# Transposing h and h2 with block DMAs and VectorE instead of TensorE, in a two-layer graph kernel on one core

## The chip, the core and the metric

The kernel runs on one core of one Trainium2 chip. The metric is the device time of one execution in microseconds, lower is better. "Before" and "after" are the medians of several executions. A run of a program on a single core is called fast unless it lies more than 1.5% above the fastest of the same kernel; all runs quoted here are fast ones.

## The reference, cut to what matters

Layer 0 normalizes x, applies a three-hop diffusion with attention weights and adds the result; layer 1 normalizes again and adds a gated value projection. B = 128 graphs, N = 128 nodes, D = 512 features, all fp32.

```python
h = jnp.maximum(_layernorm(x), 0.0)                    # "h" in the kernel
# layer 0
e = leaky_relu(sj[:, None, :] + si[:, :, None] + ab)    # sj, si from h @ Wv
transition = A * exp(e) / (sum(A * exp(e), -1) + 1e-12)
H = 0; Xk = h
for k in range(3):
    H = H + Xk @ Wk[k] + bk[k]
    Xk = transition @ Xk
x = x + relu(H)
# layer 1
h = jnp.maximum(_layernorm(x), 0.0)                    # "h2" in the kernel
q, k = split(h @ Wqk); v = h @ Wv
w = inv_scale * mask * sum(q * (adj @ (k * mask)), -1)
x = x + softmax(w, axis=1)[:, :, None] * v
```

## The kernel before

Two graphs form a pair, and there are 64 pairs. The products of a layer contract over features, and the kernel hands h and h2 to TensorE with the features on the partitions. Each layer is done as seven block products in the manner of Strassen: three banks of PSUM, each used twice or three times, with evictions on VectorE in between that set free the bank for its next product. Layer 1 of a pair runs after layer 0 of the next pair. The parts that the change touches:

```python
def transposed(h, dst):                      # h [128 nodes, 2 graphs, 512] -> features on partitions
    for j in range(G):
        pt = ps_t.tile([P, 2, HC, P], FP, name="pt")
        for c in range(DC):
            nc.tensor.transpose(pt[:, c // HC, c % HC, :], h[:, j, c * P:(c + 1) * P], ident)   # L239
        (nc.vector.tensor_copy if j else nc.scalar.copy)(dst(j), pt)                            # L240

def strassen0(p, steps):                     # layer 0; [cut: evictions of the first products]
    ...
    product(bb, 6, True)
    nc.vector.tensor_add(s[:, 2], b, s[:, 1])
    steps[0]()                               # next pair: transposed(h), attention
    product(bc, 7, True)
    product(bb, 5, False)
    nc.vector.tensor_add(s[:, 3], b, s[:, 0])          # L339 before, L360 after
    nc.vector.tensor_add(hb[:, 1, HD:], c, s[:, 3])
    steps[1]()
    product(ba, 2, False)
    nc.vector.tensor_add(hb[:, 0, :HD], a, lo)
    product(bb, 3, False)                    # reuses the bank that L339 / L360 reads
    ...

def strassen1(p):                            # layer 1
    product(a, 1, True)
    nc.scalar.copy(s[:, 0], a)
    product(b, 6, True)
    nc.vector.tensor_add(s[:, 1], b, s[:, 0])          # L364 before, L385 after
    product(c, 7, True)
    product(b, 5, False)                     # reuses the bank that L364 / L385 reads
    ...

for p in range(NP + 1):                      # [cut: first and last pairs]
    strassen0(p, steps)                      # steps: transposed(h[p+1]), attention(p+1), ...
    propagate(p + 1)
    H2[p] = norm_relu(X1[p], "h2", late["p"])
    yv = strassen1(p - 1)
    w = aggregate(p - 1, yv)
    prepare0(p + 1)
    finish(p - 1, yv, w)                     # softmax of pair p-1 and its output
    X2[p] = late["p"].tile([P, G, 2, HC, N], FP, name="x2")
    transposed(H2[p], lambda j: X2[p][:, j])
    SX2[p] = left_sums(...)                  # four sums that products 5, 6, 7, 3 need
    norm0(p + 2)
```

In the traces of this case VectorE and the queues took their instructions in the order in which a scheduler laid them down when the kernel was built, not in the order of the source. That will matter.

## Time and profile before

| | before |
|---|---|
| time, median (3 runs) | 2529.99 us (2529.98 to 2530.89) |
| TensorE busy | 99% of the span |
| one steady period (a pair) | 38.49 us |
| VectorE work in a period | 26.2 us |
| mean granted clock of TensorE | 0.995 |

In the views, PE is TensorE, PEld its weight loads, DVE VectorE, ACT ScalarE and SPq the DMA queue of the sync engine; `out<-in` names the tiles that an instruction writes and reads, and `<-` after an idle time names what ended it. The prediction below shows and reads the busy table, the chain of waits and the timeline. The first is the view of cores; the second the view by source line of the adjacency load's DMA, where the three numbers are the shortest, median and longest time in ns that an issue held its queue.

```profile
core 0: 2528.2 us, clock 0.995
```

```profile
L70 SPq DMA_DIRECT2D ag<-in_adj_dram x64: 367/368/459, 1.2 to 2327.0; - x64
```

This load out of DRAM held the queue for 0.37 us in the median, 0.46 at the most. L240 copied the transposes of h and h2 out of their `pt` tiles, 128 times on VectorE at 675 ns and 128 times on ScalarE at 586.

### The profile page before, as it was taken

What the parts mean: (1) busy time and instruction counts of PE and PEld (TensorE: products, weight loads), DVE (VectorE), ACT (ScalarE), POOL (GpSimd) and SP (SyncE); (2) the same over time, 40 slices, a digit from 0 to 9 for tenths busy, and PEclk for the clock granted to TensorE, in tenths of its full rate; (3) what the DMA queues carried; (4) which work ended last, traced back from release to release, by engine and by line L of the source; (5) the groups of instructions that cost most, each with busy time, mean ns of one, the idle gap of its engine ahead of it and who ended that gap; (6) DMA issues with size and microseconds to landing.
All of it is one profiled execution on the core that took longest, in us unless ns stands there. A gap on an engine that the chain in (4) does not pass through costs nothing.

```text
span 2528.2 us, 28170 instructions
## 1 busy us (share of the span) xinstructions
PE 2491.1 (99%) x10313; PEld 1794.9 (71%) x10313; DVE 1700.4 (67%) x4648; ACT 698.6 (28%) x1677; POOL 0.7 (0%) x6
## 2 busy tenths in 40 slices
PE   5999999999999999999999999999999999999998
PEld 4677676776776776776767767767767767677675
DVE  6666667667667666666676676676666666766764
ACT  2322222223223223222222232232232222222321
POOL 0000000000000000000000000000000000000000
PEclk8999999999999999999999999999999999999999
DMA  5110010001000100100100010001001001000000
GB/s 161 36 38 30 28 38 29 29 30 36 30 30 28 38 30 28 38 30 28 38 28 30 30 36 30 30 28 38 30 28 38 30 27 36 30 30 30 34 9 25
DMA packets 62473, 86.28 MB, mean 34 GB/s; under 512 B 3712, under 2 KB 28416, under 8 KB 62336
## 3 DMA queue, kind: packets, MB, share of 16 engines
q1 hardware_dynamic: 62336, 84.49, 10.1%
q8 instruction: 81, 1.33, 0.2%
q14 instruction: 56, 0.46, 0.1%
HBM read 50.92 MB, written 33.55 MB: 33 GB/s over the span
## 4 chain that ended last, share of the span: by engine, by line
PE 96%; issue 0%; DVE 0%; ACT 0%; DVEq 0%; ACTq 0%
PE pm L313 75%; PE pt L293 8%; PE pt L239 4%; PE pt L383 4%; PE pt L124 1%; PE pt L281 1%; PE pt L277 1%; PE pt L266 1%; ACT h L216 0%; DVE junk L386 0%; DVE x L409 0%; ACT ej L400 0%; DVE yv L374 0%; DVEq L478 0%; DVE w L397 0%
## 5 line engine op out<-in xcount | busy, mean ns | idle before, releaser
L313 PE MATMUL pm<-t,sx 128*128 128x256 f32 x2304 | 518.6, 379 | 0.1
L313 PEld LDWEIGHTS pm<-t,sx 128*128 128x128 f32 x2304 | 432.6, 190 | 56.4 <-DVE sx L302 0.3
L313 PE MATMUL pm<-b,x 128*128 128x256 f32 x1536 | 390.8, 380 | 0.0
L313 PE MATMUL pm<-f,sx 128*128 128x512 f32 x768 | 340.1, 592 | 0.0
L313 PEld LDWEIGHTS pm<-b,x 128*128 128x128 f32 x1536 | 267.6, 191 | 55.2 <-issue 30.1
L295 ACT COPY x<-pt 128x512 f32<-128x512 f32 x256 | 147.6, 576 | 488.3 <-PE pt L293 488.3
L313 PEld LDWEIGHTS pm<-f,sx 128*128 128x128 f32 x768 | 145.6, 190 | 184.2 <-issue 150.2
L313 PE MATMUL pm<-e,x 128*128 128x512 f32 x512 | 240.6, 592 | 0.0
L293 PE MATMUL pt<-tt,h 128*128 128x256 f32 x1024 | 233.9, 382 | 0.5 <-ACT tt L282 0.5
L293 PEld LDWEIGHTS pt<-tt,h 128*128 128x128 f32 x1024 | 196.1, 192 | 27.9 <-ACT tt L282 0.8
L216 ACT ACTIVATE h<-x,rs 128x512 f32<-128x512 f32 x128 | 97.3, 807 | 290.1 <-PE pt L383 278.5
L313 PE MATMUL pm<-b,sx 128*128 128x256 f32 x768 | 176.2, 379 | 0.0
L313 PE MATMUL pm<-t,x 128*128 128x256 f32 x768 | 176.2, 379 | 0.0
L231 DVE SCALAR_TENSOR_TENSOR junk<-h,u_bc 128x512 f32<-128x512 f32 x256 | 174.4, 684 | 1.8 <-ACT h L216 1.8
L313 PEld LDWEIGHTS pm<-e,x 128*128 128x128 f32 x512 | 97.3, 190 | 95.6 <-issue 92.1
L313 PEld LDWEIGHTS pm<-b,sx 128*128 128x128 f32 x768 | 145.9, 190 | 19.8
L313 PEld LDWEIGHTS pm<-t,x 128*128 128x128 f32 x768 | 145.9, 190 | 19.8
L216 ACT ACTIVATE h<-xg,rs 128x512 f32<-128x512 f32 x128 | 97.1, 806 | 175.3 <-DVE rs L213 175.3
L239 PE MATMUL pt<-ident,h 128*128 128x128 f32 x1024 | 144.7, 274 | 0.7 <-ACT h L216 0.5
L240 ACT COPY x<-pt 128x512 f32<-128x512 f32 x128 | 75.1, 586 | 248.1 <-PE pt L239 242.3
L239 PEld LDWEIGHTS pt<-ident,h 128*128 128x128 f32 x1024 | 122.6, 142 | 14.1 <-ACT h L216 1.4
L372 DVE TENSOR_TENSOR yv<-pm,s 128x512 f32<-128x512 f32 x64 | 44.3, 692 | 129.0 <-PE pm L313 129.0
(105 smaller groups left out, 2844.9 us busy)
## 6 DMA issues: line engine op xcount, KB each, us to landing
xg<-in_x_dram SPq DMA_DIRECT2D x64, 512.0 KB, 3.5
out_dram<-x SPq DMA_DIRECT2D x64, 512.0 KB, 2.8
ag<-in_adj_dram SPq DMA_DIRECT2D x64, 128.0 KB, 2.1
b<-in_L_gnn_Wk_dram SPq DMA_DIRECT2D x12, 256.0 KB, 5.9
w<-in_L_gnn_Wqk_dram SPq DMA_DIRECT2D x8, 256.0 KB, 5.3
wv_sb<-in_L_gnn_Wv_dram SPq DMA_DIRECT2D x1, 1024.0 KB, 7.5
e<-in_L_gnn_Wv_dram SPq DMA_DIRECT2D x4, 256.0 KB, 6.1
bk_bc<-in_L_gnn_bk_dram SPq DMA_DIRECT2D x3, 256.0 KB, 5.8
```

The costliest lines, as they stand in the source:

```text
L124: nc.tensor.transpose(dst, col.to_broadcast([P, P]), ident)
L216: nc.scalar.activation(h[:, j, :], src[:, j, :], AF.Relu, bias=rs[:, 1, j:j + 1], scale=rs[:, 0, j:j + 1])
L231: nc.vector.scalar_tensor_tensor(junk, h[:, j, :], 1.0, u_bc[:, a, :], op0=OP.mult, op1=OP.mult, accum_out=s[:, j, a:a + 1])
L239: nc.tensor.transpose(pt[:, c // HC, c % HC, :], h[:, j, c * P:(c + 1) * P], ident)
L240: (nc.vector.tensor_copy if j else nc.scalar.copy)(dst(j), pt)
L266: nc.tensor.transpose(pa[:, j, :], a[:, j, :], ident)
L277: nc.tensor.transpose(pt[:, j, :], t[:, j, :], ident)
L293: nc.tensor.matmul(pt[:, c].rearrange("p k n -> p (k n)"), h[:, j, at:at + P], tt[:, j].rearrange("p k n -> p (k n)"), start=True, stop=True)
L295: nc.scalar.copy(X[p][:, j, kh, 1:3].rearrange("p k c n -> p c k n"), pt)
L313: nc.tensor.matmul(bank[:, :width], left[i][:, c * P:(c + 1) * P], right[i][:, c], start=(first and c == 0), stop=(c == n - 1), skip_group ...
L372: nc.vector.tensor_add(o[0][1], b, s[:, 0])
L383: nc.tensor.matmul(pa, at[:, j, :], h2[:, j, :], start=True, stop=True)
```

## The change

The intent is to take the transposes off TensorE, the engine that bounds the kernel (96% of the chain that ended last). DMAs move 32-row blocks between partitions, in runs of 512 bytes, and VectorE finishes the transposition within blocks of 32x32. The features then come out in a permuted order, and the rows of the weights are loaded in the same order to match. Besides, the softmax of a pair (`finish`) is moved into layer 0 of the pair after next, where its two small matmuls need not wait for VectorE (before, their weight loads waited 20.4 us in all).

```diff
     def transposed(h, dst):
-        for j in range(G):
-            pt = ps_t.tile([P, 2, HC, P], FP, name="pt")
+        hv = front.tile([P, Q, G, P], FP, name="hv", bufs=1)
+        for n in range(Q):                                   # Q = 4, DC = 4: 16 DMAs
             for c in range(DC):
-                nc.tensor.transpose(pt[:, c // HC, c % HC, :], h[:, j, c * P:(c + 1) * P], ident)
-            (nc.vector.tensor_copy if j else nc.scalar.copy)(dst(j), pt)
+                nc.sync.dma_start(hv[c * S32:(c + 1) * S32, n],              # L255
+                                  h[n * S32:(n + 1) * S32, :, c * P:(c + 1) * P])
+        for j in range(G):
+            nc.vector.transpose(dst[:, j].rearrange("p f (n b) -> p f n b", n=Q),   # L258
+                                hv[:, :, j].rearrange("p n (f a) -> p f n a", f=Q))
...  (weight rows loaded in the permuted order; layout of x; one junk buffer instead of two)
-                steps = (lambda: (begin(n), attention(n)), lambda: t_transposed(n))
+                steps = (lambda: (begin(n), attention(n), end()), lambda: t_transposed(n))
...
-            finish(p - 1, yv, w)
+            ends.append((p - 1, yv, w))                      # end() calls finish later
```

More of the change, by code (lines that the diff above doesn't have):

```diff
@@ L44 @@
     G = 2
+    S32 = 32
+    Q = P // S32
     NP = B // G
@@ L88, with rows @@
     nc.sync.dma_start(nm, nodemask)
+    def rows(dst, w, kh):
+        for c in range(DC):
+            at = c * P + kh * HC * S32
+            nc.sync.dma_start(dst[c * S32:(c + 1) * S32],
+                              w[at:at + HC * S32].rearrange("(f a) o -> a f o", a=S32))
     def block0(pool, name, kh, nh):
         t = pool.tile([P, K, HC, HD], FP, name=name)
-        for k in range(K):
+        rows(t[:, 0], wk[0, :, nh * HD:(nh + 1) * HD], kh)
+        for k in range(1, K):
             src = wk[k, kh * HD:(kh + 1) * HD, nh * HD:(nh + 1) * HD]
@@ L113 @@
             e[kh, nh] = pool.tile([P, HC, 2, HD], FP, name=f"e{kh}{nh}")
-            src = wv1[kh * HD:(kh + 1) * HD, nh * HD:(nh + 1) * HD]
-            nc.sync.dma_start(e[kh, nh][:, :, 1, :], src.rearrange("(c p) o -> p c o", p=P))
+            rows(e[kh, nh][:, :, 1, :], wv1[:, nh * HD:(nh + 1) * HD], kh)
     ident = const.tile([P, P], FP, name="ident")
@@ L131 @@
         for c in range(DC):
-            junk = front.tile([P, D], FP, name="junk")
+            junk = front.tile([P, D], FP, name="junk", bufs=1)
             nc.vector.scalar_tensor_tensor(junk, wv0_sb[:, c, :], 1.0, aw_bc[:, a, :],
@@ L138 @@
         nc.vector.tensor_copy(u_bc[:, a, :], pu.rearrange("p c i -> p (c i)"))
-        junk = front.tile([P, D], FP, name="junk")
+        junk = front.tile([P, D], FP, name="junk", bufs=1)
         nc.vector.scalar_tensor_tensor(junk, bv_bc, 1.0, aw_bc[:, a, :],
@@ L184, in score_matrix @@
                 t = wpool.tile([P, D], FP, name=f"wt{a}")
-                (nc.vector.tensor_copy if a else nc.scalar.copy)(t, p.rearrange("p c i -> p (c i)"))
+                if a:
+                    nc.vector.tensor_copy(t, p.rearrange("p c i -> p (c i)"))
+                else:
+                    nc.scalar.copy(t.rearrange("p (f c a) -> p f c a", f=Q, c=DC),
+                                   p.rearrange("p c (f a) -> p f c a", f=Q))
                 wt.append(t)
@@ L229, in norm0 @@
             for a in range(2):
-                junk = front.tile([P, D], FP, name="junk")
+                junk = front.tile([P, D], FP, name="junk", bufs=1)
                 nc.vector.scalar_tensor_tensor(junk, h[:, j, :], 1.0, u_bc[:, a, :], op0=OP.mult,
@@ L234, in transposed @@
     def transposed(h, dst):
+        hv = front.tile([P, Q, G, P], FP, name="hv", bufs=1)
+        for n in range(Q):
+            for c in range(DC):
+                nc.sync.dma_start(hv[c * S32:(c + 1) * S32, n],
+                                  h[n * S32:(n + 1) * S32, :, c * P:(c + 1) * P])
         for j in range(G):
-            pt = ps_t.tile([P, 2, HC, P], FP, name="pt")
-            for c in range(DC):
-                nc.tensor.transpose(pt[:, c // HC, c % HC, :], h[:, j, c * P:(c + 1) * P], ident)
-            (nc.vector.tensor_copy if j else nc.scalar.copy)(dst(j), pt)
+            nc.vector.transpose(dst[:, j].rearrange("p f (n b) -> p f n b", n=Q),
+                                hv[:, :, j].rearrange("p n (f a) -> p f n a", f=Q))
     def attention(p):
@@ L294, in propagate @@
                                      tt[:, j].rearrange("p k n -> p (k n)"), start=True, stop=True)
-                nc.scalar.copy(X[p][:, j, kh, 1:3].rearrange("p k c n -> p c k n"), pt)
-    def left_sums(blocks, pool, name, width, bufs):
-        s = pool.tile([P, 4, width], FP, name=name, bufs=bufs)
-        a = [[blocks[:, j, kh] for kh in range(2)] for j in range(G)]
-        nc.vector.tensor_add(s[:, 0], a[1][0], a[1][1])
-        nc.vector.tensor_sub(s[:, 1], s[:, 0], a[0][0])
-        nc.vector.tensor_sub(s[:, 2], a[0][0], a[1][0])
-        nc.vector.tensor_sub(s[:, 3], a[0][1], s[:, 1])
+                nc.scalar.copy(X[p][:, 1:3, j, kh].rearrange("p k c n -> p c k n"), pt)
@@ L305, in left_sums @@
+    def left_sums(a, pool, name, width):
+        s = pool.tile([P, 4] + width, FP, name=name, bufs=1)
+        nc.vector.tensor_add(s[:, 0], a[1, 0], a[1, 1])
+        nc.vector.tensor_sub(s[:, 1], s[:, 0], a[0, 0])
+        nc.vector.tensor_sub(s[:, 2], a[0, 0], a[1, 0])
+        nc.vector.tensor_sub(s[:, 3], a[0, 1], s[:, 1])
         return dict(zip((5, 6, 7, 3, 1, 2, 4),
-                        [s[:, 0], s[:, 1], s[:, 2], s[:, 3], a[0][0], a[0][1], a[1][1]]))
-    def products(left, right, width):
+                        [s[:, 0], s[:, 1], s[:, 2], s[:, 3], a[0, 0], a[0, 1], a[1, 1]]))
@@ L310, in product, with products @@
+    def products(left, right):
         def product(bank, i, first):
-            n = left[i].shape[1] // P
-            for c in range(n):
-                nc.tensor.matmul(bank[:, :width], left[i][:, c * P:(c + 1) * P], right[i][:, c],
-                                 start=(first and c == 0), stop=(c == n - 1), skip_group_check=True)
+            _, n, m = left[i].shape
+            chunks = [(k, c) for k in range(n) for c in range(m // P)]
+            for at, (k, c) in enumerate(chunks):
+                r = right[i][:, k, c]
+                nc.tensor.matmul(bank[:, :r.shape[-1]], left[i][:, k, c * P:(c + 1) * P], r,
+                                 start=(first and at == 0), stop=(at == len(chunks) - 1),
+                                 skip_group_check=True)
@@ L315, in products @@
         return product
-    R0 = {i: t.rearrange("p k c o -> p (k c) o") for i, t in right0.items()}
     def prepare0(p):
-        SX[p] = left_sums(X[p].rearrange("p j h k c n -> p j h (k c n)"), front, "sx", K * HD, 1)
+        a = {(j, kh): X[p][:, :, j, kh].rearrange("p k c n -> p k (c n)")
+             for j in range(G) for kh in range(2)}
+        SX[p] = left_sums(a, front, "sx", [K, HD])
     def strassen0(p, steps):
-        product = products(SX.pop(p), R0, HD)
+        product = products(SX.pop(p), right0)
@@ L353, in strassen1 @@
     def strassen1(p):
-        product = products(SX2.pop(p), R1, D)
+        product = products(SX2.pop(p), R1)
         X2.pop(p)
@@ L383, in aggregate @@
             nc.tensor.matmul(pa, at[:, j, :], h2[:, j, :], start=True, stop=True)
-            junk = front.tile([P, D], FP, name="junk")
+            junk = front.tile([P, D], FP, name="junk", bufs=1)
             b = p * G + j
@@ L413, in begin @@
     def begin(p):
-        X[p] = front.tile([P, G, 2, K, HC, N], FP, name="x")
-        transposed(H[p], lambda j: X[p][:, j, :, 0])
-    nothing = (lambda: None, lambda: None)
+        X[p] = front.tile([P, K, G, 2, HC, N], FP, name="x")
+        transposed(H[p], X[p][:, 0].rearrange("p j h c n -> p j (h c) n"))
     norm0(0)
@@ L425, with end @@
     R1 = None
-    W = {}
+    ends = []
+    def end():
+        while ends:
+            finish(*ends.pop())
     for p in range(NP + 1):
@@ L430 @@
                 n = p + 1
-                steps = (lambda: (begin(n), attention(n)), lambda: t_transposed(n))
+                steps = (lambda: (begin(n), attention(n), end()), lambda: t_transposed(n))
             else:
-                steps = nothing
+                steps = (end, lambda: None)
             strassen0(p, steps)
@@ L436 @@
                 propagate(p + 1)
+        else:
+            end()
         if p == 0:
@@ L439 @@
             setup_ctx.close()
-            R1 = {i: t.rearrange("p c k o -> p c (k o)") for i, t in right1.items()}
+            R1 = {i: t.rearrange("p (s c) k o -> p s c (k o)", s=1) for i, t in right1.items()}
             late["p"] = ctx.enter_context(tc.tile_pool(name="late", bufs=1))
@@ L449 @@
         if p > 0:
-            finish(p - 1, yv, w)
+            ends.append((p - 1, yv, w))
         if p < NP:
             X2[p] = late["p"].tile([P, G, 2, HC, N], FP, name="x2")
-            transposed(H2[p], lambda j: X2[p][:, j])
-            SX2[p] = left_sums(X2[p].rearrange("p j h c n -> p j h (c n)"), late["p"], "sx2", HD, 1)
+            transposed(H2[p], X2[p].rearrange("p j h c n -> p j (h c) n"))
+            a = {(j, kh): X2[p][:, j, kh:kh + 1].rearrange("p k c n -> p k (c n)")
+                 for j in range(G) for kh in range(2)}
+            SX2[p] = left_sums(a, late["p"], "sx2", [1, HD])
         if p + 2 < NP:
             norm0(p + 2)
+    end()
 _INS = ['x', 'adj', 'nodemask', 'L0_gnn_Wv', 'L0_gnn_bv', 'L0_gnn_aw', 'L0_gnn_ab', 'L0_gnn_Wk',
```

## The prediction

Its 0.65 us for a transpose of 512 elements a partition on VectorE is the author's estimate: the trace before had other work of that size at 0.68 us, with the next start after 0.6, and no such transpose.

> **What bounds the kernel now.** I read the busy table of the page first, then the chain of waits that ended last, then the timeline of one pair in the middle of the run.
>
> ```profile
> PE 2491.1 (99%) x10313; PEld 1794.9 (71%) x10313; DVE 1700.4 (67%) x4648; ACT 698.6 (28%) x1677; POOL 0.7 (0%) x6
> ...
> PE 96%; issue 0%; DVE 0%; ACT 0%; DVEq 0%; ACTq 0%
> PE pm L313 75%; PE pt L293 8%; PE pt L239 4%; PE pt L383 4%; PE pt L124 1%; PE pt L281 1%; PE pt L277 1%; PE pt L266 1%; ACT h L216 0%; DVE junk L386 0%; DVE x L409 0%; ACT ej L400 0%; DVE yv L374 0%; DVEq L478 0%; DVE w L397 0%
> ...
> L239 PE MATMUL pt<-ident,h 128*128 128x128 f32 x1024 | 144.7, 274 | 0.7 <-ACT h L216 0.5
> ```
>
> TensorE carries 96% of the chain. L239, the transposes of h and h2, is 4% of it, about 100 us; that is what the change takes away. Busy time alone would mislead, because matmul records overlap. So I took distances between starts in a steady stretch:
>
> ```profile
> 1206.25 1.04 PE L239 MATMUL pt<-ident,h 128*128 128x128 f32 x8
> 1207.12 0.38 PE L124 MATMUL pt<-ident,s 128*128 128x128 f32 x2
> ```
>
> Eight transposes occupy 0.87 us, or 0.109 us each, not the 274 ns of the row. The two groups of four in the same pair take 0.43 us each, so one pair (8 for h2, 8 for h) spends 1.73 us. The same way: 84 records of 256 columns at 0.2155 us are 18.1 us (twelve take 2.59), 28 of 512 columns 12.0, L383 1.7, L293 3.45, and twelve small ones about 1.3. With L239 that is 38.3 us. The windows view of one whole period says
>
> ```profile
> 1200.08:1238.57 38.49, 38.49 (x161) 27.82 (x160) 26.16 (x73) 10.81 (x27) 0.00 (x0) 1.00 0.10 32
> ```
>
> so TensorE has nothing to spare: 64 such periods of 38.49 us are 2463 of 2530 us, and the rest is start and end. What I could not place, some 0.1 us a pair, lies at the softmax's `spread`, which waits for the aggregation on VectorE:
>
> ```profile
> PEld pt L124 <- DVE junk L386: 20.4, 65, 1.5
> ```
>
> VectorE has 26.2 us of work in a period, but it is not slack everywhere. The second eviction of layer 1 gates a product:
>
> ```profile
> 1221.38 0.42 DVE L347 TENSOR_TENSOR x<-pm,s 128x256 f32<-128x256 f32 x1 [0.49 <-PE pm L313]
> ...
> 1228.68 0.68 DVE L364 TENSOR_TENSOR s<-pm,s 128x512 f32<-128x512 f32 x1
> 1229.41 0.19 PEld L313 LDWEIGHTS pm<-f,sx 128*128 128x128 f32 x1 [0.30 <-DVE s L364]
> ```
>
> From L347, which TensorE releases, to the end of L364 VectorE works 7.98 us without a pause, and the weight load that needs L364 starts only 0.05 us behind its 0.43 us rhythm. That stretch is the second most important fact here: each 0.1 us added to it is added to the period.
>
> [...]with the overhead of other 512-element work (BATCH_NORM_STATS2 0.68 us, next start after 0.6) I estimate 0.65 us. No transpose on VectorE is in this trace. [...]the trace's 128 KB adj load, in 512-byte runs, lands in 2.1 us.
>
> **The change part by part.**
> 1. *TensorE transposes.* They leave: 1.73 us a pair.
> 2. *Softmax moved.* The instruction order of the built kernel has the two `spread` matmuls of pair p-1 after the second product of layer 0 of pair p+1, 5 us after the aggregation ended. The 0.1 us wait goes; the tensor work stays. Together 1.83 us a pair: 38.49 becomes 36.66 if nothing new waits, over some 63 pairs 115 us.
> 3. *DMAs.* 16 of 32 KB per transposition, 32 a pair. An issue took 0.37 us on the sync queue, start to start 0.5 us in the first ones (0.74 to 1.23 us); I take 0.42 to 0.5 us. Sixteen take 7 to 8 us, and landing adds 2: 9 to 10 us from h to all blocks. The queue is then busy 15 of 37 us. The DMA engines get 2048 packets of 512 B more a pair; at the mean of all packets now (10.1% of 16 engines' 2528 us over 62336 packets, 65 ns) that is 8.4 us of each engine, a load of a third rather than a tenth: no bound.
>  *h2:* with layer 0's first product at 0, ScalarE finishes h2 at about 1.7, the blocks land at 10.5 to 12. VectorE, following its new order (aggregation 0.9, dot products, z, exp, both output updates), comes to these transposes at 10.7. The eviction behind them is needed by the product that starts at 14.3; it would end at about 12.5 to 13.8. Hidden.
>  *h of the next pair:* there is one hv buffer, so its DMAs start when the h2 transposes have been read, at 12.3, and land at 21 to 22.5. VectorE reaches these transposes at 22.2, after the last eviction of layer 0 (19.7) and 2.5 us of normalization. Just hidden, with about 0.5 us to spare at the middle.
> 4. *VectorE.* 4 transposes of 0.65 come, 2 copies of 0.675 go: 26.2 to about 27.4 of 36.7 us, 75%. But two transposes fall inside the tight stretch, 1.25 to 1.3 us. In the built order one of the four layer-0 sums (0.87 to 0.95) and some small operations of the other norm (0.2 to 0.3) have moved behind the eviction. Adding pitches, 2.48 before the transposes, 1.28, and 4.33 after them give 8.09, where 7.98 is now just enough. I charge 0.15 us a pair, 9 us.
> 5. *ScalarE.* Two copies a pair less, off the path.
> 6. *Start.* 20 more load DMAs, then 16 for h, on one queue: about 45 issues at 0.5 us, so h's blocks land near 38 to 41 us. Layer 0 of pair 0 starts at 41.87 now, its sums at 42.04. The built order also places pair 1's propagation (3.5 us) ahead of it in time that is idle now. I estimate 4 us gained.
> 7. *End.* The last layer 1 has nothing to hide behind: h2, 16 issues, landing and a transpose are 11 us where about 3 pass now (2503 to 2506.2). 8 us lost.
> Sum: 2530 - 115 + 9 - 4 + 8 = 2428; a little for block transfers that come late in some pairs makes 2432.
>
> **The rivals.**
> (a) *The blocks of h come late.* If a DMA costs 0.55 us to issue, or lands in 3 us, they land at 23 to 24.5, VectorE stands in front of them and the gating eviction slips by 1 to 2 us a pair: 60 to 120 us back, ending at 2490 to 2540. For it: one queue, one buffer, a wait on all eight DMA semaphores. Against it: 0.37 us of issue in all later DMAs, small transfers with no HBM in them.
> (b) *VectorE becomes the bound of the tight stretch.* If a transpose of 4-byte data takes 1.2 us rather than 0.65, two add 1.1 us a pair, some 70 us: about 2500. For it: no such instruction in the trace. [...]
> (c) *The transposes were hidden anyway.* Then nothing changes. Against it: the periods add up to TensorE's own pitches, and L239 is 4% of the chain.
>
> **Range and chances.** Without any stall about 2418 to 2423; with 0.15 us a pair 2430; with 0.8 us, 2470. I give (a) or (b) in such a size that under 2% is left about one chance in eight, and hardly any chance to be slower, as the loss would have to exceed 2.6 us a pair. Predicted 2432 us, range 2416 to 2474, faster 0.87, within 2% 0.11, slower 0.02.
>
> **What would show it.** Right: L239's row gone, a period of 36.7 to 36.9 us in the timeline, TensorE still above 97% busy, VectorE transposes near 0.65 us, no wait of VectorE on the hv DMAs over 0.3 us a pair, a sync queue with 0.42 to 0.5 us from start to start, first layer 0 near 42 us, last gap near 11 us. Wrong: a period above 37.5 with VectorE waiting for the hv DMAs (rival a), or without that wait but with weight loads waiting for the second eviction of layer 1 (rival b), or a period still at 38.5 (rival c).

## More of the kernel before

The granted clock is the share of its full clock that TensorE was given.

TensorE was granted 0.995 of its clock in the mean, and was busy in 99% of the span.

## The result

After: 2817.09 us, median of 4 runs (2800.19 to 2822.92). Before, on the same chip: 2530.3 us. The kernel became 11% slower: the ratio is 1.1122, with a 95% interval from 1.1074 to 1.1171. Ratios here are the mean time of one kernel's fast runs over that of the other's of the same rounds, so they are not quite the ratio of the medians.

The page of the kernel after: busy table, then the chain that ended last by engine and by line.

```profile
PE 2509.6 (89%) x9289; PEld 1727.5 (61%) x9289; DVE 1787.3 (63%) x4776; ACT 637.7 (23%) x1549; POOL 0.7 (0%) x6
...
SPq 40%; PE 24%; DVE 14%; DMA 8%; issue 7%; ACT 3%; DVEq 0%; ACTq 0%
SPq L255 40%; PE pm L333 20%; DMA hv<-h 8%; DVE x L258 6%; PE pt L404 4%; ACT h L231 3%; DVE sx L319 2%; DVE sx L321 2%; DVE s L385 1%; DVE st L216 1%; DVE s L360 1%; DVEq L258 0%; DVE rs L228 0%; DVE mv L217 0%; DVE sx L320 0%
```

Before, TensorE carried 96% of this chain. Now the sync engine's queue carries 40%, all of it on the one line that issues the block DMAs. The queue holds the chain with issuing and not with moving bytes, which is 8% of it. TensorE has 1024 matmuls fewer (9289 for 10313) and yet more busy time, which is odd.

The waits of the kernel after (engine, who waits, for what: us in total, times, longest):

```profile
DVE x L258 <- DMA hv<-h: 449.1, 127, 8.0
...
PE pm L333 <- DVE s L385: 193.2, 62, 4.2
```

VectorE waits 449 us for blocks, about 3.5 us at each of its two places in a pair. TensorE waits for the second eviction of layer 1 (L385) in almost every pair, 3.1 us each time, and 60.4 us in all for L360 of layer 0. Now the timeline of one pair: start, duration, what, and in brackets the idle time before it. First h2, whose layer 0 starts on TensorE at 1323.59.

```profile
1325.34 10.17 SPq L255 DMA_DIRECT2D hv<-h  x16
...
1337.00 1.31 DVE L258 STREAM_TRANSPOSE x<-hv 128x512 f32<-128x512 f32 x2 [3.11 <-DMA hv<-h]
1338.23 0.39 DVE L360 TENSOR_TENSOR s<-pm,s 128x256 f32<-128x256 f32 x1
1338.33 6.99 SPq L255 DMA_DIRECT2D hv<-h  x11
...
1338.67 2.86 PE L333 MATMUL pm<-b,sx 128*128 128x256 f32 x12 [0.64 <-DVE s L360]
```

Sixteen issues take 10.17 us, 0.64 us from start to start. VectorE came to the transposes at 1333.89 and waited 3.11 us; L360 stands behind them on the same engine, and TensorE stopped for it. Only when the transposes had been read, at 1338.3, could the DMAs of h begin in the one buffer. They are the second load on the same chain; here is where the blocks of an h, issued in the same way one pair earlier, arrive:

```profile
1307.64 1.31 DVE L258 STREAM_TRANSPOSE x<-hv 128x512 f32<-128x512 f32 x2 [3.39 <-DMA hv<-h]
...
1312.47 0.68 DVE L385 TENSOR_TENSOR s<-pm,s 128x512 f32<-128x512 f32 x1
...
1313.20 2.78 PE L333 MATMUL pm<-f,sx 128*128 128x512 f32 x4 [2.95 <-DVE s L385]
...
1315.78 2.82 PE L333 MATMUL pm<-e,x 128*128 128x512 f32 x4
...
1318.44 1.88 PE L333 MATMUL pm<-e,sx 128*128 128x512 f32 x4
```

VectorE loses 3.39 us at the transposes, which stand in the stretch that was tight already; L385 slips, and TensorE stops 2.95 us. And it is not only the stop. The four matmul records after it take 2.78 and 2.82 us, where four of the same size take 1.88 a little later. The weight loads show the rhythm:

```profile
1315.78 0.34 PEld L333 LDWEIGHTS pm<-e,x 128*128 128x128 f32 x1 [0.52 <-issue]
1316.63 0.34 PEld L333 LDWEIGHTS pm<-e,x 128*128 128x128 f32 x1 [0.52 <-issue]
...
1318.01 0.19 PEld L333 LDWEIGHTS pm<-e,sx 128*128 128x128 f32 x1 [0.24 <-issue]
...
1318.44 0.19 PEld L333 LDWEIGHTS pm<-e,sx 128*128 128x128 f32 x1 [0.24 <-issue]
```

From about 1 us after the stop they are 0.85 us apart, and from 1318.01 on 0.43 again: for some 3.4 us TensorE ran at half its clock. Eight matmuls from 1313.20 to 1318.44 took 5.24 us instead of 8 x 0.43 = 3.44, so this stop cost another 1.8 us. The view of cores has the sum of it:

```profile
core 0: 2817.7 us, clock 0.955
```

A mean of 0.955 over 2817.7 us is 127 us of clock lost; before, 0.995 of 2528.2 us is 13. That explains why TensorE with less to do was busy longer. But stops and half clock do not go one to one. The trace's record of the granted clock has 49 stretches at half clock, most of them of 3.41 us or double that, and all begin on one grid of 3.41 us. Of the 62 stops for L385, 42 have such a stretch at their end and 20 have none. A stop of 2.95 us that ended at 376.78, as long as the one above, has none. The windows view of the two (start:end, length, then busy time of PE, PEld, DVE, ACT and POOL, and the clock) shows why:

```profile
372.18:375.59 3.41, 1.65 (x4) 0.38 (x2) 3.41 (x10) 0.00 (x0) 0.00 (x0) 1.00 0.20 75
375.59:379.00 3.41, 2.22 (x5) 1.06 (x6) 2.71 (x9) 0.50 (x2) 0.00 (x0) 1.00 0.00 0
...
1310.84:1314.25 3.41, 1.04 (x3) 0.57 (x4) 3.27 (x9) 0.11 (x1) 0.00 (x0) 1.00 0.00 0
1314.25:1317.66 3.41, 3.41 (x6) 1.35 (x5) 2.19 (x7) 1.91 (x4) 0.00 (x0) 0.50 0.00 0
```

A line of the grid cuts the first stop in two, so that TensorE stood 1.76 us in one window of the grid and 1.19 us in the next; in the second case it stood 2.37 us in one window, and the window after that was granted half. Between 100 us and the last 60 us of the run, all 42 windows at full clock in which TensorE stood for more than 2.0 us were followed by one at half clock, and none of those under 1.89 us was. None of these windows was wholly idle; the longest idle time in one was 3.07 us. So half clock is a matter of how a stop lies on the grid, too. From 125 to 2745 us the stretches at half clock add up to 222 us; TensorE stood in 25 of them, and half of the other 197 us, 98 us, were lost: 1.6 us a pair in the mean.

The whole difference can be split at two points that both kernels have, the first aggregation matmuls (L383 before, L404 after) of pair 0 and of the pair 61 periods later, read from the timelines:

| us of the span | before | after |
|---|---|---|
| start, up to the first aggregation | 120.51 | 130.99 |
| 61 periods | 2347.74 (38.49 each) | 2614.38 (42.86 each) |
| the rest | 59.95 | 72.33 |

Of the 289.5 us between the spans 266.6 are in the periods. A period was meant to be 36.66; of the 6.2 us above that, 3.1 are TensorE's wait for L385, 1.0 its wait for L360 and 1.6 the half clock after the stops; some 0.5 us are not placed.

### The profile page after: what moved, and what is told of

It reads as the page before. It is cut to its first block, busy times and chain, and to the rows that moved or that the text cites. A ratio compares the mean times of both kernels' runs of the same rounds, so it can differ in the third digit from the quotient of the medians.

```text
span 2817.7 us, 29462 instructions
## 1 busy us (share of the span) xinstructions
PE 2509.6 (89%) x9289; PEld 1727.5 (61%) x9289; DVE 1787.3 (63%) x4776; ACT 637.7 (23%) x1549; POOL 0.7 (0%) x6
## 4 chain that ended last, share of the span: by engine, by line
SPq 40%; PE 24%; DVE 14%; DMA 8%; issue 7%; ACT 3%; DVEq 0%; ACTq 0%
SPq L255 40%; PE pm L333 20%; DMA hv<-h 8%; DVE x L258 6%; PE pt L404 4%; ACT h L231 3%; DVE sx L319 2%; DVE sx L321 2%; DVE s L385 1%; DVE st L216 1%; DVE s L360 1%; DVEq L258 0%; DVE rs L228 0%; DVE mv L217 0%; DVE sx L320 0%
## 5 line engine op out<-in xcount | busy, mean ns | idle before, releaser
L333 PE MATMUL pm<-f,sx 128*128 128x512 f32 x768 | 418.9, 688 | 193.2 <-DVE s L385 193.2
L258 DVE STREAM_TRANSPOSE x<-hv 128x512 f32<-128x512 f32 x256 | 167.0, 690 | 452.6 <-DMA hv<-h 449.1
L333 PE MATMUL pm<-b,x 128*128 128x256 f32 x1536 | 362.8, 379 | 0.0
L333 PEld LDWEIGHTS pm<-b,x 128*128 128x128 f32 x1536 | 282.3, 190 | 60.1 <-issue 30.1
L333 PE MATMUL pm<-e,x 128*128 128x512 f32 x512 | 274.4, 663 | 11.1 <-DVE x L258 11.1
L314 ACT COPY x<-pt 128x512 f32<-128x512 f32 x256 | 148.6, 580 | 566.7 <-PE pt L312 566.7
L333 PE MATMUL pm<-b,sx 128*128 128x256 f32 x768 | 189.1, 398 | 60.4 <-DVE s L360 60.4
L333 PEld LDWEIGHTS pm<-e,x 128*128 128x128 f32 x512 | 116.4, 228 | 145.1 <-issue 121.1
L221 ACT ACTIVATE r<-mv,eps 128x2 f32<-128x2 f32 x128 | 37.9, 296 | 437.3 <-DVE mv L217 435.5
L404 PE MATMUL pt<-h,aT 128*128 128x512 f32 x256 | 120.5, 592 | 0.5 <-ACT h L231 0.5
L333 PE MATMUL pm<-e,sx 128*128 128x512 f32 x256 | 120.3, 592 | 0.0
## 6 DMA issues: line engine op xcount, KB each, us to landing
wv_sb<-in_L_gnn_Wv_dram SPq DMA_DIRECT2D x1, 1024.0 KB, 10.2
```

The costliest lines, as they stand in the source:

```text
L221: nc.scalar.activation(r[:, 0], var, AF.Ln, bias=eps)
L258: nc.vector.transpose(dst[:, j].rearrange("p f (n b) -> p f n b", n=Q), hv[:, :, j].rearrange("p n (f a) -> p f n a", f=Q))
L314: nc.scalar.copy(X[p][:, 1:3, j, kh].rearrange("p k c n -> p c k n"), pt)
L333: nc.tensor.matmul(bank[:, :r.shape[-1]], left[i][:, k, c * P:(c + 1) * P], r, start=(first and at == 0), stop=(at == len(chunks) - 1), sk ...
L404: nc.tensor.matmul(pa, at[:, j, :], h2[:, j, :], start=True, stop=True)
```

## The experiments

**My theory:** the blocks are late, because 16 issues on one queue take 10.2 us; VectorE works in order, so it stands in front of an eviction that TensorE needs; TensorE's stop then brings half clock with it in many pairs. **The rivals:** VectorE's transposes themselves are too much for the tight stretch; the moved softmax does harm; the added traffic disturbs other transfers; and, later, the number of DMAs on one queue costs this time wherever VectorE stands.

### 1. No block DMAs (result wrong)

```diff
-        hv = front.tile([P, Q, G, P], FP, name="hv", bufs=1)
-        for n in range(Q):
-            for c in range(DC):
-                nc.sync.dma_start(hv[...], h[...])
...
-                                hv[:, :, j].rearrange("p n (f a) -> p f n a", f=Q))
+                                h[:, j, :].rearrange("p (n f a) -> p f n a", n=Q, f=Q))
```

> The changed kernel with the 32 block DMAs a pair taken out: VectorE transposes straight from h and h2, so blocks stay in their place and the output is wrong on purpose. All else, VectorE's transposes included, stays. Theory A (the block DMAs come late: 0.6 us of issue each on one queue): with them gone a pair takes about 36.7 to 36.9 us, the run 2405 to 2440 us, TensorE over 97% busy, granted clock 0.99. Rival B (the VectorE transposes lengthen VectorE's tight stretch and hold the second eviction of layer 1): still above 2500 us with weight loads waiting for that eviction.

2410.13 us (2409.81 to 2410.45), ratio to before 0.9521 [0.9502, 0.954]. The result is wrong, as meant (relative error 0.199): the blocks were never moved between partitions. The page and the view of cores:

```profile
PE 2374.5 (99%) x9289; PEld 1693.6 (70%) x9289; DVE 1771.2 (74%) x4776; ACT 624.0 (26%) x1549; POOL 0.7 (0%) x6
```

```profile
core 0: 2408.7 us, clock 0.999
```

All 256 VectorE transposes are there, and TensorE is at 99% with its full clock; 61 periods take 36.66 us each, the number of the prediction. So the transposes do no harm by themselves and 407 us hang on the DMAs. One limit: without the DMAs the scheduler laid VectorE's order down differently, and the transposes no longer stood in the tight stretch. The sixth experiment has them there.

### 2. The moved softmax alone, on the kernel before

```diff
-                steps = (lambda: (begin(n), attention(n)), lambda: t_transposed(n))
+                steps = (lambda: (begin(n), attention(n), end()), lambda: t_transposed(n))
...
-            finish(p - 1, yv, w)
+            ends.append((p - 1, yv, w))
```

> The kernel before with the softmax move alone. Theory A: the wait of 0.1 us a pair goes, 2518 to 2530 us. Rival C (the moved softmax puts VectorE and ScalarE work in front of the layer-0 evictions and costs time): above 2560 us.

2532.13 us (2531.14 to 2533.2), ratio 1.0003 [0.9988, 1.0018]. Nothing lost and nothing gained. The 0.1 us a pair that I had counted for it is not to be seen.

### 3. A second buffer for h2's blocks

```diff
-    def transposed(h, dst):
-        hv = front.tile([P, Q, G, P], FP, name="hv", bufs=1)
+    def transposed(h, dst, pool=front, name="hv"):
+        hv = pool.tile([P, Q, G, P], FP, name=name, bufs=1)
...
-            transposed(H2[p], X2[p].rearrange(...))
+            transposed(H2[p], X2[p].rearrange(...), late["p"], "hv2")
```

> The changed kernel with one hv buffer for h and another for h2. In its built order h's sixteen DMAs come first and h2's queue behind them. Theory A: h's blocks are early, VectorE's wait in front of the second eviction of layer 1 (3.9 us of weight-load wait a pair) goes; but h2's DMAs start some 4 us after h2 is ready and land near 16 us after layer 0's start, so the eviction behind the h2 transposes is 3 to 3.5 us late: 2640 to 2730 us in all. Rival B (VectorE's work) or D (the DMA traffic slows the engines): within 2% of the changed kernel, 2760 to 2830 us, as the work and the traffic are the same.

2732.69 us (2729.73 to 2735.66), ratio 1.0795 [1.0773, 1.0816]. Nearly a third of the loss came back, a little less than I expected. Timeline of one pair, whose layer 0 starts at 1328.02:

```profile
1321.12 20.46 SPq L255 DMA_DIRECT2D hv<-h  x32
```

```profile
1342.96 1.30 DVE L258 STREAM_TRANSPOSE x<-hv 128x512 f32<-128x512 f32 x2 [4.19 <-DMA hv<-h]
1344.18 0.39 DVE L360 TENSOR_TENSOR s<-pm,s 128x256 f32<-128x256 f32 x1
```

With the buffer free, the queue issues the 16 DMAs of h first, and those of h2 after them, in one go of 20.46 us. The wait at h is gone in this pair, and its place is taken by a longer one at h2: VectorE stands 4.19 us before L360, and TensorE's waits for L360 rise to 172.1 us. The buffer was a real constraint, but the bottleneck under it is the queue.

### 4. More work for TensorE in the stop

Three matmuls whose result nobody reads, between products 7 and 5 of layer 1:

```diff
         product(c, 7, True)
+        fill = ps_t.tile([P, D], FP, name="pt")
+        for i in range(3):
+            nc.tensor.matmul(fill, ident, u_bc[:, 0, :], start=True, stop=True)
         product(b, 5, False)
```

> The changed kernel with three more matmuls of 512 columns (six records, 2.6 us at full clock) whose result nobody reads, put where TensorE stands and waits for the second eviction of layer 1. Theory A with the clock (a stop of some 3 us halves TensorE's clock for the next 3.4 us, 254 us of the trace at half clock): the work fills the stop, the clock stays up, and the run gets shorter by 60 to 120 us, 2700 to 2760, with a granted clock over 0.985. If the clock is only a by-product: no change, 2800 to 2825. If the filler adds its time: about 2980.

2728.96 us (2727.99 to 2731.21), ratio to before 1.0782 [1.0764, 1.08]; against the kernel after it is 88 us faster, with more to do. The timeline around the stop, and the view of cores:

```profile
1319.18 2.74 PE L389 MATMUL pt<-u_bc,ident 128*128 128x512 f32 x6
...
1322.32 1.98 PE L333 MATMUL pm<-f,sx 128*128 128x512 f32 x4 [0.40 <-DVE s L385]
```

```profile
core 0: 2726.7 us, clock 0.994
```

The dummies fill the stop, 0.40 us of it are left, the next four records take 1.98 and not 2.78 us, and the granted clock is 0.994 again. The waits of TensorE for L385 fall by 154 us (193.2 to 39.1), and the dummies themselves take about as much, some 2.6 us a pair; so the 88 us are the clock, by this count. VectorE waits for blocks as before (458.0 us in 128 waits). So the half clock after a stop is a cost of its own, and no part of the lateness.

### 5. The traffic alone, on the kernel before

After h and h2 are ready, 32 DMAs a pair copy pieces of them into a tile that nobody reads. Three shapes take turns by pair: 32 partitions with two runs of 512 bytes (as in the change), 32 with one of 1 KB, and 128 with one of 512 bytes.

```diff
...
+                if kind == 0:
+                    nc.sync.dma_start(dz[d, n].rearrange("p (j f) -> p j f", j=G), h[f, :, c * P:(c + 1) * P])
+                elif kind == 1:
+                    nc.sync.dma_start(dz[d, n], h[f, 0, :2 * P])
+                else:
+                    nc.sync.dma_start(dz[:, n], h[:, 0, c * P:(c + 1) * P])
...
```

> The kernel before, with 32 SBUF-to-SBUF DMAs a pair issued beside it from the sync queue, out of h and h2 into a scratch tile that nobody reads. Three shapes in turn, by pair: a) 32 partitions of 2 pieces of 512 bytes, as in the changed kernel; b) 32 partitions of one piece of 1024 bytes; c) 128 partitions of one piece of 512 bytes. Theory A (traffic is harmless, only lateness costs): 2525 to 2550 us. Rival D (the traffic itself slows TensorE's or VectorE's reads): above 2600 us, with longer matmul pitch. For the issue time: if it goes with the number of 512-byte pieces, b is shorter than a's 0.60 us and c much longer; if it is a fixed price of a DMA from SBUF to SBUF, all three are near 0.60 us.

2532.43 us, ratio 1.0002 [0.9982, 1.0022]. The traffic does no harm: the DMA engines are loaded to 23.2% instead of 10.1%, and nothing else slows. The issue times by source line, of the first and of the second shape:

```profile
L253 SPq DMA_DIRECT2D dza<-h x688: 585/595/1642, 92.1 to 2517.8; - x172
```

```profile
L255 SPq DMA_DIRECT2D dzb<-h x656: 507/589/1990, 128.2 to 2447.6; - x164
```

The third has a median of 598 ns. So these DMAs within SBUF held the queue for 0.589 to 0.598 us in the median, with one run or two in each partition, over 32 partitions or 128; in the kernel after, the first of a burst (0.59 us at 1325.34) did so like the others (0.595 in the median). None of the three shapes helped; whether fewer DMAs do is the next experiment.

### 6. Fewer DMAs, through DRAM

h goes to DRAM whole in one DMA and comes back by blocks in four: 10 issues a pair instead of 32.

```diff
...
-        hv = front.tile([P, Q, G, P], FP, name="hv", bufs=1)
-        for n in range(Q):
-            for c in range(DC):
-                nc.sync.dma_start(hv[c * S32:(c + 1) * S32, n],
-                                  h[n * S32:(n + 1) * S32, :, c * P:(c + 1) * P])
+        hv = front.tile([P, G, Q, P], FP, name="hv", bufs=1)
+        hd = dram.tile([G, Q, S32, D], FP, name="hd")
+        nc.sync.dma_start(hd.rearrange("j n a d -> (n a) j d"), h)
+        for c in range(DC):
+            nc.sync.dma_start(hv[c * S32:(c + 1) * S32].rearrange("a j n f -> a (j n) f"),
+                              hd[:, :, :, c * P:(c + 1) * P].rearrange("j n a f -> a (j n) f"))
...
```

> The changed kernel with the 16 block DMAs of a transposition replaced by five: one writes h whole to DRAM, four read it back by blocks into the one hv buffer. More bytes cross the HBM, but the sync queue issues 10 instead of 32 a pair. Theory A (the number of issues on one queue): blocks of h2 land about 9 to 10 us after layer 0's start, those of h near 18, both ahead of VectorE; 2420 to 2450 us, TensorE over 96% busy, clock over 0.99. Rival: if it is the round trip and not the issue that costs, blocks come later than before (two landings in a row) and the run stays above 2650 us.

Correct, 2427.77 us (2425.9 to 2429.3), ratio to before 0.9588 [0.9574, 0.9602]: **4.1% faster than before and the best version.** Issues of the two lines, then the chain by engine and the transposes' row of the page:

```profile
L255 SPq DMA_DIRECT2D hd<-h x128: 360/377/472, 35.5 to 2394.9; - x128
```

```profile
L257 SPq DMA_DIRECT2D hv<-hd x512: 302/444/1637, 39.1 to 2399.0; - x171
```

```profile
PE 97%; DVE 1%; DMA 1%; SPq 0%; ACT 0%; issue 0%; DVEq 0%; ACTq 0%
...
L260 DVE STREAM_TRANSPOSE x<-hv 128x512 f32<-128x512 f32 x256 | 165.3, 683 | 3.7 <-DMA hv<-hd 3.5
```

The four reads take 1.85 us of the queue in the period read, not 10.2. They move more bytes (the mean traffic rises from 55 to 91 GB/s) and land later, 2.8 us after issue where the direct ones take 1.9, behind a write that itself takes 3.4 us to land; and it does not matter: VectorE waits 3.5 us for them in the whole run. A period is 36.64 us. The transposes of h stand in the tight stretch of layer 1 here, 1.29 us of them, and TensorE does not wait for the eviction behind them. That settles the rival about VectorE.

### 7. The same with a second buffer

```diff
-            transposed(H2[p], X2[p].rearrange(...))
+            transposed(H2[p], X2[p].rearrange(...), late["p"], "hv2")
```

> As the DRAM bounce, with an hv buffer each for h and h2. The built order then puts the transposes of h in front of the last eviction of layer 0 rather than behind it. Theory A: little is left to gain, within 15 us of the run with one buffer, 2415 to 2450 us. If the one buffer was still a wait there: 20 to 60 us faster than it.

2433.21 us (2432.16 to 2435.14), ratio 0.9609 [0.9593, 0.9625]. The second buffer brings nothing once the queue is short; it is no faster than with one.

### 8. Every second block DMA from GpSimd

```diff
-                nc.sync.dma_start(hv[c * S32:(c + 1) * S32, n],
+                (nc.sync, nc.gpsimd)[c % 2].dma_start(hv[c * S32:(c + 1) * S32, n],
```

> The changed kernel with every second block DMA issued by the idle GpSimd's queue: same DMAs, same bytes, half the issues on the sync queue (5 us a transposition). The built order also changes: the h2 transposes stand in front of the exponent's product. Theory A: if GpSimd needs no more than 1 us for each, the blocks land 8 to 11 us after h is ready, and the run falls to 2480 to 2680 us. Rival (landing, not issue, is what is late): no change, 2780 to 2830 us.

2576.93 us (2573.86 to 2580.01), ratio 1.0178 [1.0157, 1.0198]. The same 32 DMAs with the same bytes, issued from two queues (0.54 us each on GpSimd's, 0.60 on the sync engine's), give 240 us back. What is left is partly another wait: 110.3 us of TensorE for the attention's weights, behind h2's transposes on VectorE. So most of the time was lost in issuing and not in the transfers; the built order of VectorE changed along with the queues, so that the 240 us are not the issuing alone.

### 9. The transposes later on VectorE

With two buffers and all 32 DMAs on one queue, one-element copies into the output force h2's transposes, which stood in front of L360, behind the eviction of product 3. In the built order those of h now stand behind the eviction of product 7.

```diff
...
         nc.vector.tensor_add(hb[:, 0, HD:], b, s[:, 0])
+        if p:
+            nc.vector.tensor_copy(X2[p - 1][:, 0, 0, 0, :1], hb[:, 0, HD:HD + 1])
+            nc.vector.tensor_copy(X2[p - 1][:, 1, 0, 0, :1], hb[:, 0, HD:HD + 1])
+            sums1(p - 1)                     # h2's transposes and the four sums
         product(bc, 4, False)
...
```

> Correct. The 32 SBUF-to-SBUF DMAs a pair with their two buffers stay as in the run with two buffers (20.5 us of the queue a pair); only the place of the VectorE transposes moves: the built order now has those of h behind the evictions that reuse products 5 and 7 of layer 0, and those of h2 (with their four sums) behind the eviction of product 3 (a one-element copy of that eviction's result into their output forces it; 4 small VectorE copies). Theory A (a late block costs time only because VectorE, in order, stands in front of an eviction that TensorE needs): no wait of VectorE on the hv DMAs in front of those evictions, TensorE above 97% of the span, granted clock above 0.99, 2420 to 2480 us, although the queue is as busy as before. Rival D (32 issues a pair on one queue are too many wherever VectorE uses the blocks, so only fewer issues help, as in the run through DRAM): waits of VectorE on hv stay at 3 us or more a pair and pass to TensorE; 2600 us or more. In between (2480 to 2600): blocks of h2, which land some 15.5 us after layer 0 begins, are still late for layer 1 in part of the pairs.

2693.19 us (2689.63 to 2694.44), ratio 1.0634 [1.0616, 1.0652]. That is what the rival expected, and my theory missed it by more than 200 us. The timeline of one pair (layer 0 starts at 1315.02):

```profile
1310.78 20.75 SPq L255 DMA_DIRECT2D hv<-h  x32
```

```profile
1332.87 1.31 DVE L259 STREAM_TRANSPOSE x<-hv 128x512 f32<-128x512 f32 x2 [5.75 <-DMA hv<-h]
1334.10 0.39 DVE L366 TENSOR_TENSOR x<-pm,bsum 128x256 f32<-128x256 f32 x1
```

VectorE waits 5.75 us, and this time for h. The instruction order of the built kernel told why: the scheduler had put 13 of h's DMAs, then all 16 of h2's, and then the last 3 of h on the queue. h was ready first, but its last blocks landed after the 32nd issue. So the run did not decide between the two theories.

### 10. The same, with all of h's DMAs first

h's DMAs are put down in the source as soon as h exists, ahead of those of h2, and its transposes are held behind the eviction of product 7 in the same way.

```diff
         if p + 2 < NP:
             norm0(p + 2)
+            BLOCKS[p + 2] = transposed(H[p + 2])          # the 16 DMAs alone
+        if p < NP:
+            LATER2[p] = transposed(H2[p], late["p"], "hv2")
...
+    def x_blocks(p):
+        if p:
+            for j in range(G):
+                nc.vector.tensor_copy(X[p][:, 0, j, 0, 0, :1], X1[p - 1][:, 1, HD:HD + 1])
...
```

> Correct. As the run with the transposes moved later (32 SBUF-to-SBUF DMAs a pair on one queue, two buffers), but with the order of the queue put right: there the built order put the last 3 block DMAs of h behind all 16 of h2, so that h's blocks landed after the 32nd issue; here all 16 of h stand first, then the 16 of h2, and the h transposes are held behind the second eviction of bank b's partner (product 7) by a one-element copy. Estimate from that run's times, with layer 0's first product at 0: h issues from -4 to 6 and lands at 8, VectorE comes to it at 12; h2 issues from 6 to 16.4 and lands at 18.3, VectorE comes to it at 17. So only some 1 to 1.5 us of waiting a pair are left, at the transposes of h2, of which the tight stretch of layer 1 can give back about 1.3. Theory A (what counts is when the last block lands against where VectorE stands): waits of VectorE on hv under 2 us a pair, granted clock over 0.98, 2430 to 2530 us. Rival D (32 issues on one queue cost the same in any order): 2600 us or more.

Correct, 2498.33 us (2495.84 to 2500.51), ratio to before 0.9873 [0.9856, 0.9889]: 1.3% faster than before, and 319 us faster than after, with the same 32 DMAs of the same shape on the same queue. Its page, its waits for blocks, and TensorE at the place where it used to stop:

```profile
PE 2394.7 (96%) x9289; PEld 1694.2 (68%) x9289; DVE 1788.2 (72%) x5028; ACT 641.6 (26%) x1549; POOL 0.7 (0%) x6
```

```profile
DVE x L259 <- DMA hv<-h: 51.9, 80, 8.0
```

```profile
1248.23 1.98 PE L335 MATMUL pm<-f,sx 128*128 128x512 f32 x4 [0.25 <-DVE s L391]
```

The waits for blocks fall from 449.1 to 51.9 us, TensorE's stops to a fraction of a microsecond in most pairs, and the clock is 0.995 again: in no window of the grid does TensorE stand for more than 1.5 us in the same part of the run. So 32 issues on one queue do not cost the time by their number. They cost it where the last one lands after VectorE has come to stand in front of an eviction. The rest against the version through DRAM is mostly a period of 37.67 us instead of 36.64; TensorE waits 46.9 us for the second eviction of layer 1 (0.76 us a pair); h2's transposes and sums, which now stand just ahead of the tight stretch, are the likely cause, but no run tried that.

## Why the prediction was wrong, point by point

It said 2432 us and was off by 385, on the side to which it had given 2 chances in 100. The step that failed is the third of these points.

1. **TensorE's transposes, 1.73 us a pair: right.** L239 is gone, and without lateness a period is 36.64 us (experiment 6), where the prediction had 36.66.
2. **The softmax's 0.1 us: not found** (experiment 2). With 36.64 measured, the two terms together were right to 0.02 us; how they share it was not.
3. **The DMAs: this is the step that failed.** Its term was 0.42 to 0.5 us an issue, so 7 to 8 us for sixteen. Measured: 0.595 us held and 0.64 from start to start, so 10.2 us. The prediction took the issue time from lone loads and from the loads at the start, all out of DRAM; these DMAs are within SBUF. The landing, 2 us assumed where the trace before had 2.1 for the adjacency load, was right (1.9). The term was used twice in a row, because of the one buffer: h2's blocks came 13.4 us after layer 0 began, not at 10.5 to 12; h's DMAs could start at 14.7, not 12.3; and its blocks came some 26.4 us after layer 0 began, not at 21 to 22.5. An error of 2 to 3 us in one burst became 4 to 5 us at the end. That the DMA engines themselves would be no bound was right: they were busy 19% of the time, where the prediction had a third.
4. **Where VectorE comes to the transposes: right to 1 us.** Predicted at 10.7 and 22.2, measured at 10.3 and, in the pair read, 23.1. The prediction worked with a slack of 0.5 us at h as "just hidden", and gave one chance in eight to all the ways in which it might not hold.
5. **The duration of a transpose: right**, 0.69 us for an estimate of 0.65; and two of them fit into the tight stretch (experiment 6), so rival (b) fell. The 0.15 us a pair that the prediction charged there did not show either, with a period of 36.64 us.
6. **Rival (a) was the mechanism, with the size too small.** "If a DMA costs 0.55 us to issue", it said, 1 to 2 us a pair or 60 to 120 us back. The waits of TensorE alone are 3.1 + 1.0 us a pair. The prediction let h's blocks arrive at 23 to 24.5; they arrived 2 us later. Its own sign of rival (a), a period above 37.5 us with VectorE waiting for the blocks, is what the trace shows.
7. **Missing altogether: the clock.** No term stood for what TensorE does after a stop. It was about 98 us, 1.6 us a pair in the mean though only 42 of the 62 stops for L385 brought it; experiment 4, which filled the stop, got 88 us back.
8. **The start was wrong in sign.** 4 us gained were predicted; up to the first aggregation the kernel after needs 10.5 us more. Behind the added loads, the DMAs of the first h began only at 36.91, and VectorE had its blocks at 48.82, where 38 to 41 were predicted; the first layer 0 began at 53.32, not near 42. The version through DRAM, whose first layer 0 begins within 1 us of the same moment and which has no late blocks, needs 3.7 more. Pair 1's work does stand ahead of the first layer 0, as the prediction had seen, but the time there was not idle time to be had for nothing: TensorE waits for VectorE inside it, 3.68 and 3.17 us at a time.
9. **The end was right**: TensorE's gap before the last layer 1 is 11.1 us, predicted 11.

Rival (c), that the transposes were hidden anyway, is refuted by the 4.1% of experiment 6. **What stays open:** why the DMAs within SBUF held the queue for 0.595 us where those out of DRAM took 0.444 in experiment 6; the runs exclude only the three shapes tried and the place in the burst. And the gain of experiment 6 comes from fewer issues and from an order of VectorE that the scheduler changed along with them; experiment 10 shows that with all 32 issues left on the queue, order, landing time and a second buffer are worth 319 us, where experiment 6 won 389.

## What to carry to other kernels

Count the DMA issues on a queue as work on an engine, with a start-to-start time measured in bursts of the same kind; sixteen small ones were a 10 us instruction here. The queue was held for 0.368 us by a lone load out of DRAM, 0.377 by a write of h to DRAM, 0.444 by a read out of DRAM in a burst of four and 0.595 within SBUF, where it was 0.64 from start to start. VectorE should not stand waiting for a transfer in front of something that the bounding engine needs: its waits for blocks were 449.1 us in the kernel after and 51.9 in experiment 10. Check in the built order both of the engine and of the queue, for in experiment 9 the scheduler had put the last three DMAs of one group behind sixteen of another. And the stops of TensorE, some 3 us each, cost more than their length here where half clock came after them, and that was after 42 of the 62.
